# Layer 0 of a four-layer graph attention stack: biases as TensorE products, row copies on ScalarE, later input copies issued from the SP queue

## The chip, the cores and the metric

One core of one Trainium2 chip. The metric is the device time of one execution in microseconds: the median of 3 executions. The kernel before takes 3261.68 us (3260.0 to 3262.12). The profiled execution has a span of 3261.5 us.

## What is computed

The input is `x`, 3327 nodes with 256 features in f32, and one adjacency matrix of 3327 x 3327 integers, the same for four layers. Some 1% of its entries are ones, and each row has at most a few dozen. Every layer is graph attention with a residual and a layer norm. The change lies in layer 0, whose scores are of the kind in which the nonlinearity sits inside the sum over features:

```python
g_src = nodes @ W_src_w.T + W_src_b
g_tgt = nodes @ W_tgt_w.T + W_tgt_b
g = leaky_relu(g_src[:, None, :] + g_tgt[None, :, :], 0.2)
score = where(adj_mat != 0, einsum('ijc,c->ij', g, a_w), -inf)
x = layernorm(x + softmax(score, axis=1) @ g_tgt)
# layers 1 to 3: other forms of attention over the same adj, each with residual and layernorm
```

## The kernel before

**Layer 0 works on lists of neighbours.** `sparse0` (from L250) never forms the dense scores. For each node it finds the column numbers of the ones in its adjacency row (at most 56), sorts nodes by their number of neighbours, and gathers the target rows of the neighbours, k-th neighbour by k-th neighbour for 128 nodes at a time. A gather is an indirect DMA issued by POOL (L527), 923 of them for the layer.

**Tiles and sets.** The nodes are 26 tiles of 128 rows (the last has 127). They are grouped in three sets of 5, 9 and 12 tiles (`SETS`). Within a set, the nodes are ranked by their neighbour count over all the set's tiles, so that a later tile of the ranked order needs fewer gathers (`LEVELS`).

**Tables in DRAM.** `table_d` holds a target row of 260 floats for each node: `g_tgt` (256), in column 256 its share of the score that is linear in the target, and zeros. `own_d[s]`, one per set, holds what a node needs of itself: minus `g_src` (columns 0 to 255), its input row of x (256 to 511), and its target row (512 on). The copies of x into the middle columns are DRAM-to-DRAM transfers issued by POOL at L312, before anything else of the layer uses them; `copy_rows` (L104) cuts each into a multiple of 16 rows and a remainder, which makes four transfers.

**Three generators feed the tables.** `targets(it)` (L332) loads 128 columns of x transposed on SP (L322), multiplies them on TensorE into `pt` (PSUM, two buffers), then VectorE adds the bias, replicated over all partitions in `bt_row`, into `row` (L343), ScalarE copies the one column 256 (L344), and ScalarE's queue issues the two writes to the tables (L345, L346). A memset on VectorE zeroes the columns from 256 on (L336). `sources(it)` (L349) does likewise with `w_src` into `pss` (one buffer); VectorE computes `-pss - bias` in one instruction (L359), and ScalarE's queue issues the write (L363). `neighbours(s)` (L376) does the ranking of one set: for each tile it loads two halves of 128 adjacency rows on SP (L396, two `adj_i` buffers; it shows as L110, the line in `copy_rows`), turns the ones into descending numbers (L402), takes the eight largest of each chunk of 64 (L421), and then the largest 56 of what is left (L433, L435). It makes a key from the count, and TensorE replicates the keys of the tile over the partitions (`key_rows`, L466). After all tiles, L475 counts for each node how many keys are larger, and L479 makes these the ranks. `neighbours` itself advances `sources`, at half of the chunks of each half.

**The order of the work.** Within `sparse0`, TensorE, VectorE, ScalarE and POOL run in the order in which the program is written (`manual_schedule`, L259 to L266); SP isn't in this list. The first phase (L720) writes, in turn, one tile of `targets` and one step of `neighbours(0)`, then the rest of `neighbours(0)`. POOL then scatters the neighbour lists to their ranks (`write_list`, L488) and reads them back (L496). After that a loop over all parts (groups of up to 8 gathers, L770) writes for each part: as many steps of `neighbours(1)` and `neighbours(2)` as are due (L771 to L776), gathers four parts ahead, and `score`, with `combine` at the end of a tile. `lay_out` (L537) brings a node's own source row and `a_row` to PSUM on ScalarE, which also scales the gathered rows by their weights (L633); TensorE adds the scaled rows up (L636). So VectorE's single queue holds the ranking of the later sets and the scores of the current one, and POOL's holds the gathers and, when a set is ranked, its list writes.

**Afterwards.** `layers` (L973) runs layers 1 to 3, dense, on TensorE above all. If a row had more neighbours than the lists hold, a dense fallback would run (L1441); it doesn't with these inputs. One statement outside the layers is of use below: the memset of `most` at L1435, near the end of the program.

Of the kernel before, what the change touches and what calls it, by code (L numbers as in the profile page):

```python
# [8 lines left out]
F32 = mybir.dt.float32  # L9
# [5 lines left out]
ALU = mybir.AluOpType  # L15
# [4 lines left out]
P = 128  # L20
# [12 lines left out]
SETS = (5, 9, 12)  # L33
# [8 lines left out]
ROW = 260  # L42
# [4 lines left out]
def gat_stack(  # L47
# [29 lines left out]
    nc = tc.nc  # L77
    n, dim = x.shape
    nt = -(-n // P)
    kc = dim // P  # L80
# [23 lines left out]
    def copy_rows(engine, dst, src):  # L104

        rows = dst.shape[0]
        whole = rows // 16 * 16
        for lo, hi in ((0, whole), (whole, rows)):
            if lo < hi:
                engine.dma_start(dst[lo:hi], src[lo:hi])  # L110
# [7 lines left out]
    def load_row(work, src, name):  # L118

        size = src.shape[0]  # L120
        t = work.tile([P, size], F32, tag="row_" + name, name=name, bufs=1)
        nc.sync.dma_start(
            t, bass.AP(tensor=src.tensor, offset=src.offset, ap=[[0, P], [1, size]])
        )
        return t
# [124 lines left out]
    def sparse0(lost):  # L250
        GROUP, TURNS, LEAD = 8, 11, 4
        starts = [sum(SETS[:s]) for s in range(len(SETS))]
        with ExitStack() as s0:
            const0 = s0.enter_context(tc.tile_pool(name="s_const", bufs=1))
# [10 lines left out]
                )  # L265
            )  # L266

            w_tgt = const0.tile([P, kc, dim + 1], F32, name="w_tgt0")
            nc.sync.dma_start(w_tgt[:, :, :dim], w_tgt_t.rearrange("(c p) f -> p c f", p=P))
            a_row = load_row(const0, a_w, "a_row")  # L270
            bt_row = load_row(const0, b_tgt, "bt_row")
            w_src = const0.tile([P, kc, dim], F32, name="w_src0")
            nc.scalar.dma_start(w_src, w_src_t.rearrange("(c p) f -> p c f", p=P))
            bs_row = load_row(const0, b_src, "bs_row")
            for c in range(kc):
                t = io0.tile([P, dim], F32, tag="hs", name="dots0")
                nc.vector.tensor_mul(t, w_tgt[:, c, :dim], a_row)
# [4 lines left out]
            ones = const0.tile([P, P], F32, name="ones")  # L282
# [4 lines left out]
            for lo, hi in halves:  # L287
                hi = -(-hi // P) * P
# [19 lines left out]
            own_d = []  # L308
            for s, size in enumerate(SETS):
                lo, hi = starts[s] * P, min(n, (starts[s] + size) * P)  # L310
                own_d.append(dram.tile([size * P, OWN], F32, name=f"own{s}_d"))
                copy_rows(nc.gpsimd, own_d[s][: hi - lo, dim : 2 * dim], x[lo:hi, :])  # L312

            def own_rows(it):
                s = max(s for s in range(len(SETS)) if starts[s] <= it)
                at0 = (it - starts[s]) * P
                return own_d[s][at0 : at0 + P, :]

            def columns_of(it):
                pn = rows_of(it)  # L320
                xt = io0.tile([P, kc, P], F32, tag="xt", name="xt", bufs=4)
                nc.sync.dma_start(xt[:, :, :pn], x_t_p[:, :, it * P : it * P + pn])  # L322
                return xt, pn

            def project(p, xt, pn, weight):
                for k in range(kc):
                    nc.tensor.matmul(
                        p[:pn, : weight.shape[2]], xt[:, k, :pn], weight[:, k, :],
                        start=(k == 0), stop=(k == kc - 1),
                    )  # L330

            def targets(it):  # L332

                xt, pn = columns_of(it)
                row = io0.tile([P, ROW], F32, tag="row", name="row", bufs=3)
                nc.vector.memset(row[:, dim:], 0.0)  # L336
                if pn < P:
                    nc.vector.memset(row[:, :dim], 0.0)
                    nc.vector.memset(row[:, dim : dim + 1], -FAR)
                pt = ps0.tile([P, BANK], F32, tag="acc", name="pt")  # L340
                project(pt, xt, pn, w_tgt)
                yield
                nc.vector.tensor_add(row[:pn, :dim], pt[:pn, :dim], bt_row[:pn])  # L343
                nc.scalar.copy(row[:pn, dim : dim + 1], pt[:pn, dim : dim + 1])  # L344
                nc.scalar.dma_start(table_d[it * P : (it + 1) * P, :], row)  # L345
                nc.scalar.dma_start(own_rows(it)[:, 2 * dim :], row)  # L346
                yield

            def sources(it):  # L349

                xt, pn = columns_of(it)
                pss = ps0.tile([P, BANK], F32, tag="ps", name="pss", bufs=1)
                project(pss, xt, pn, w_src)
                yield
                minus = io0.tile([P, dim], F32, tag="minus", name="minus")
                if pn < P:
                    nc.vector.memset(minus, 0.0)
                    nc.scalar.dma_start(own_rows(it)[pn:, dim : 2 * dim], minus[pn:])
                nc.vector.scalar_tensor_tensor(  # L359
                    minus[:pn], pss[:pn, :dim], -1.0, bs_row[:pn],  # L360
                    op0=ALU.mult, op1=ALU.subtract,
                )
                nc.scalar.dma_start(own_rows(it)[:, :dim], minus)  # L363
                yield

# [10 lines left out]
            def neighbours(s):  # L376
# [8 lines left out]
                for t in range(size):  # L385
                    it = starts[s] + t
                    pn = rows_of(it)
                    before, of_rows = of_rows, sources(it)
                    cand = io0.tile([P, len_c, 8], F32, tag="cand", name="cand")
                    sums = io0.tile([P, 4], F32, tag="sums", name="sums")  # L390
# [95 lines left out]
            def write_list(s, t):  # L486
                ranks_i, payloads = placed[s]
                nc.gpsimd.indirect_dma_start(  # L488
                    out=lists_d[s][:, :],
                    out_offset=bass.IndirectOffsetOnAxis(ap=ranks_i[:, t : t + 1], axis=0),  # L490
                    in_=payloads[t][:, :], in_offset=None,
                )

            def read_lists(s):
                lst = io0.tile([P, max(SETS), KMAX + 2], U32, tag="lst", name="lst")
                nc.gpsimd.dma_start(  # L496
                    lst[:, : SETS[s], :], lists_d[s].rearrange("(t p) k -> p t k", p=P)
                )
                listed[s] = lst
# [221 lines left out]
            for it in range(nt):  # L721
                for _ in targets(it):
                    pass
                next(first, None)
# [27 lines left out]
            for it in range(SETS[0]):  # L752
                write_list(0, it)
            read_lists(0)


            ahead, owed, steps = [], {}, 0
# [665 lines left out]
    lost = nodes.tile([P, 2 * nt], F32, name="lost")  # L1423
    nc.vector.memset(lost, 0.0)
    sparse0(lost)
    with ExitStack() as rs:
        layers(rs)
# [75 lines left out]
```

The softmax here doesn't subtract the row's maximum and nothing guards it: scores larger than these inputs give would overflow.

## Time and profile before

| | us | share of the span |
|---|---|---|
| span | 3261.5 | |
| PE busy | 2224.4 | 68% |
| DVE (VectorE) busy | 2318.1 | 71% |
| ACT (ScalarE) busy | 741.5 | 23% |
| POOL busy | 1029.6 | 32% |
| DMA, SP's queue / POOL's queue / ScalarE's queue | | 19.8% / 16.9% / 3.2% of 16 engines |
| gathers, L527 POOL x923 | 912.6, 989 ns each | |

How to read it: the shares are means over two quite different parts. Layer 0 holds POOL's whole work; layers 1 to 3, in the second half, hold most of TensorE's. Of the stretches of layer 0:

| stretch, us | PE | DVE | ACT | POOL | DMA share |
|---|---|---|---|---|---|
| 0 to 50 | 16.48 | 25.41 | 2.40 | 7.53 | 0.74 |
| 50 to 100 | 22.61 | 43.44 | 2.07 | 0.00 | 0.67 |
| 100 to 150 | 12.74 | 45.30 | 0.96 | 3.95 | 0.46 |
| 152 to 432 | 76.32 | 248.64 | 55.19 | 180.74 | 0.54 |
| 432 to 905 | 177.63 | 458.68 | 132.38 | 349.30 | 0.53 |
| 905 to 1545 | 259.48 | 356.96 | 224.98 | 466.15 | 0.42 |

"PE", "DVE", "ACT", "POOL" and "SP" are the engines; a name with q at the end is the engine's sequencer, which issues DMAs. In a line of the timeline the columns are the start, the duration, engine, line, operation, destination and source, and the number of instructions merged; in brackets stands the idle time ahead of it and what ended it. In a line of the waits they are who waited, for whom, and then the total, the number of times and the longest.

### The profile page before, as it was taken

What the parts mean: (1) busy time and instruction counts of PE and PEld (TensorE: products, weight loads), DVE (VectorE), ACT (ScalarE), POOL (GpSimd) and SP (SyncE); (2) the same over time, 40 slices, a digit from 0 to 9 for tenths busy, and PEclk for the clock granted to TensorE, in tenths of its full rate; (3) what the DMA queues carried; (4) which work ended last, traced back from release to release, by engine and by line L of the source; (5) the groups of instructions that cost most, each with busy time, mean ns of one, the idle gap of its engine ahead of it and who ended that gap; (6) DMA issues with size and microseconds to landing.
All of it is one profiled execution on the core that took longest, in us unless ns stands there. A gap on an engine that the chain in (4) does not pass through costs nothing.

```text
span 3261.5 us, 44647 instructions
## 1 busy us (share of the span) xinstructions
PE 2224.4 (68%) x15644; PEld 1218.1 (37%) x15644; DVE 2318.1 (71%) x6589; ACT 741.5 (23%) x2002; POOL 1029.6 (32%) x1034
## 2 busy tenths in 40 slices
PE   3203332343441444343899999999999999999997
PEld 2101111121220221111478888774334444334342
DVE  6789999999975655554235642117888788899998
ACT  0003231342341343333334431110111110110110
POOL 0077657777767777774000000000000000000000
PEclk7556666666765776676699999999999999999998
DMA  7466536555435444443466753332212212212111
GB/s 216 137 141 180 169 100 150 173 157 155 112 86 109 124 111 113 113 113 91 125 199 199 201 161 93 100 99 72 63 44 68 61 46 65 63 49 57 56 47 48
DMA packets 176842, 364.21 MB, mean 112 GB/s; under 512 B 33746, under 2 KB 118964, under 8 KB 176610
## 3 DMA queue, kind: packets, MB, share of 16 engines
q1 hardware_dynamic: 96682, 183.56, 19.8%
q0 software_dynamic: 49632, 141.57, 16.9%
q10 hardware_dynamic: 30296, 36.15, 3.2%
q8 instruction: 126, 2.06, 0.3%
q14 instruction: 106, 0.87, 0.1%
HBM read 320.99 MB, written 43.58 MB: 112 GB/s over the span
## 4 chain that ended last, share of the span: by engine, by line
PE 46%; DVE 4%; DMA 2%; ACT 1%; issue 1%; DVEq 0%; SPq 0%; POOL 0%; ACTq 0%; POOLq 0%
PE acc L1198 17%; PE acc L1159 15%; PE acc L1206 8%; PE misc L1011 3%; DVE e L1075 3%; PE misc L1048 1%; DMA at_i<-in_adj_t_dram 1%; PE misc L1104 1%; DMA at<-at_d 1%; PE misc L1280 0%; PE misc L1241 0%; PE acc L636 0%; DVE stats L1355 0%; DVE h L1353 0%; ACT feat L1023 0%
## 5 line engine op out<-in xcount | busy, mean ns | idle before, releaser
L527 POOL DMA_INDIRECT g<-table_d,lst x923 | 912.6, 989 | 295.6 <-issue 268.8
L1075 DVE SCALAR_TENSOR_TENSOR e<-rate,feat,at 128x896 f32<-128x896 f32 (+4 forms) x832 | 843.1, 1078 | 67.7 <-PE acc L1206 58.4
L636 PE MATMUL acc<-g,ident 128*128 128x512 f32 (+1 forms) x934 | 454.7, 644 | 545.2 <-ACT g L633 512.7
L1198 PE MATMUL acc<-e,feat 128*32 128x384 f32 (+2 forms) x6656 | 722.8, 514 | 5.2 <-DVE e L1075 2.4
L225 POOL TENSOR_TENSOR rstds<-rstds,minus_half 128x7 f32<-128x7 f32 (+1 forms) x12 | 19.6, 1633 | 1671.7 <-DVE rstds L224 1671.7
L636 PEld LDWEIGHTS acc<-g,ident 128*128 128x128 f32 x934 | 193.3, 211 | 783.7 <-ACT g L633 561.6
L546 DVE TENSOR_TENSOR y<-g,both 128x1024 f32<-128x1024 f32 (+2 forms) x240 | 276.0, 1173 | 238.4 <-DMA g<-table_d,lst 223.5
L1206 PE MATMUL acc<-e,feat 128*32 128x384 f32 (+3 forms) x3328 | 397.5, 512 | 0.0
L1198 PEld LDWEIGHTS acc<-e,feat 128*32 128x32 f32 x6656 | 245.1, 109 | 381.8 <-issue 262.5
L633 ACT ACTIVATE g<-g,w 128x256 f32<-128x256 f32 x923 | 370.6, 494 | 0.0
L552 DVE SCALAR_TENSOR_TENSOR y<-y,both 128x256 f32<-128x256 f32 x923 | 324.5, 415 | 0.0
L1159 PE MATMUL acc<-feat,e 128*128 128x257 f32 (+2 forms) x1352 | 307.4, 381 | 0.6 <-DVE h L1173 0.6
L1159 PEld LDWEIGHTS acc<-feat,e 128*128 128x128 f32 (+2 forms) x1352 | 253.2, 190 | 39.7 <-issue 4.1
L1159 PE MATMUL acc<-feat,at 128*128 128x257 bf16 (+2 forms) x2028 | 240.9, 276 | 7.5 <-DMA at<-at_d 7.3
L466 PE MATMUL key_rows<-key_diag,ones 128*128 128x128 f32 x52 | 17.8, 440 | 314.5 <-DVE key_diag L465 259.5
L1159 PEld LDWEIGHTS <-at 128*128 128x128 bf16 (+2 forms) x2028 | 200.2, 100 | 43.9 <-DMA at<-at_d 8.0
L1075 DVE SCALAR_TENSOR_TENSOR e<-rate,feat,at_i 128x896 f32<-128x896 f32 (+2 forms) x104 | 112.2, 1081 | 143.1 <-DMA at_i<-in_adj_t_dram 109.8
L1206 PEld LDWEIGHTS acc<-e,feat 128*32 128x32 f32 (+1 forms) x3328 | 136.1, 110 | 164.2 <-issue 150.4
L421 DVE MAX8 cand<-num 128x8 f32<-128x64 uint16 x1352 | 178.9, 209 | 1.0
L542 ACT COPY both<-own_of 128x256 f32<-128x256 f32 x26 | 9.7, 374 | 602.1 <-DMA own_of<-own_d,lst 469.2
L466 PEld LDWEIGHTS key_rows<-key_diag,ones 128*128 128x128 f32 x52 | 12.1, 278 | 327.8 <-DVE key_diag L465 216.0
L1092 ACT CAST at<-at_i 128x896 bf16<-128x896 int32 (+2 forms) x104 | 92.0, 885 | 108.5 <-DMA at_i<-in_adj_t_dram 104.2
(158 smaller groups left out, 1707.5 us busy)
## 6 DMA issues: line engine op xcount, KB each, us to landing
at<-at_d SPq DMA_DIRECT2D x150, 224.0 KB
at_i<-in_adj_t_dram SPq DMA_DIRECT2D x50, 448.0 KB
adj_i<-in_adj_dram SPq DMA_DIRECT2D x25, 832.0 KB
adj_i<-in_adj_dram SPq DMA_DIRECT2D x25, 831.5 KB
g<-table_d,lst POOLq DMA_INDIRECT x923, 2.8
at<-at_d SPq DMA_DIRECT2D x75, 192.0 KB
at<-at_d SPq DMA_DIRECT2D x75, 191.8 KB
at_d<-at ACTq DMA_DIRECT2D x50, 224.0 KB
```

The source lines that it names most:

```text
L421: nc.vector.max(cand[:, lo // CHUNK + c, :], v[:, c * CHUNK : (c + 1) * CHUNK])
L527: nc.gpsimd.indirect_dma_start(out=g[:, k - k0, :], out_offset=None, in_=table_d[:, :], in_offset=bass.IndirectOffsetOnAxis(ap=entry["lst" ...
L546: nc.vector.tensor_tensor(y, rows, minus_src[:, None, :].to_broadcast([P, m, dim]), op=ALU.max)
L552: nc.vector.scalar_tensor_tensor(y, y, 1.0, a, op0=ALU.mult, op1=ALU.mult, accum_out=sc)
L633: nc.scalar.activation(rows, rows, AF.Copy, scale=w[:, k : k + 1])
L636: nc.tensor.matmul(dst, ident, rows, start=start, stop=stop)
L1011: nc.tensor.matmul(pacc[:pn, : dim + nh], ht[:, k, :pn], self.weight[:, k, :], start=(k == 0), stop=(k == kc - 1),)
L1075: nc.vector.scalar_tensor_tensor(e[:pn, : c1 - c0], self.rate[b][:pn, h_of, : c1 - c0], q, at[:pn, : c1 - c0], op0=ALU.max, op1=ALU.mult,)
L1092: nc.scalar.copy(at[:pn, :w], at_i[:pn, :w])
L1159: nc.tensor.matmul(accs[s][:pn, : dim + 1], a[:pj, s * P : s * P + pn], f[:pj, : dim + 1], start=(j == 0 and part == 0), stop=(j == nt - 1 ...
L1198: nc.tensor.matmul(accs[x][p][q : q + 32, : hi - lo], f[:pj, at0 : at0 + 32], es[at0 // hd][:pj, lo:hi], start=(j == 0), stop=(j == nt - 1),)
L1206: nc.tensor.matmul(accs[x][pairs][h_of * 32 : (h_of + 1) * 32, : hi - lo], f[:pj, dim + h_of : dim + h_of + 1].to_broadcast([pj, 32]), es[ ...
```

## The change

It has three parts.

- The biases become products. `project` takes a third, optional product of a row of ones (1 x 128) with the bias as a single row (1 x 260 or 1 x 256), accumulated into the same PSUM tile. The bias rows are loaded once to one partition instead of being replicated to 128. The target weights are widened to 260 columns with zeros, so that the product already gives the whole table row.
- ScalarE takes the rows out of PSUM. One copy of 260 columns replaces VectorE's addition, its memset of the last columns and ScalarE's one-column copy; one multiplication by -1 replaces VectorE's combined instruction for the source rows. VectorE no longer does anything in `targets` and `sources`, except for the incomplete last tile.
- Of the copies of x to the own tables, only that of set 0 stays with POOL at the start. Those of sets 1 and 2 are issued from SP, and stand in the program after the lists of set 0 are read back.

It is meant to take work from VectorE and to keep the copies of the later sets out of the start.

```diff
@@ -265,13 +265,17 @@
                 )
             )
 
-            w_tgt = const0.tile([P, kc, dim + 1], F32, name="w_tgt0")
+            w_tgt = const0.tile([P, kc, ROW], F32, name="w_tgt0")
             nc.sync.dma_start(w_tgt[:, :, :dim], w_tgt_t.rearrange("(c p) f -> p c f", p=P))
+            nc.vector.memset(w_tgt[:, :, dim:], 0.0)
             a_row = load_row(const0, a_w, "a_row")
-            bt_row = load_row(const0, b_tgt, "bt_row")
+            bt_row = const0.tile([1, ROW], F32, name="bt_row")
+            nc.vector.memset(bt_row, 0.0)
+            nc.sync.dma_start(bt_row[:, :dim], b_tgt[None])
             w_src = const0.tile([P, kc, dim], F32, name="w_src0")
             nc.scalar.dma_start(w_src, w_src_t.rearrange("(c p) f -> p c f", p=P))
-            bs_row = load_row(const0, b_src, "bs_row")
+            bs_row = const0.tile([1, dim], F32, name="bs_row")
+            nc.sync.dma_start(bs_row, b_src[None])
             for c in range(kc):
                 t = io0.tile([P, dim], F32, tag="hs", name="dots0")
                 nc.vector.tensor_mul(t, w_tgt[:, c, :dim], a_row)
@@ -309,7 +313,8 @@
             for s, size in enumerate(SETS):
                 lo, hi = starts[s] * P, min(n, (starts[s] + size) * P)
                 own_d.append(dram.tile([size * P, OWN], F32, name=f"own{s}_d"))
-                copy_rows(nc.gpsimd, own_d[s][: hi - lo, dim : 2 * dim], x[lo:hi, :])
+                if s == 0:
+                    copy_rows(nc.gpsimd, own_d[s][: hi - lo, dim : 2 * dim], x[lo:hi, :])
 
             def own_rows(it):
                 s = max(s for s in range(len(SETS)) if starts[s] <= it)
@@ -322,26 +327,28 @@
                 nc.sync.dma_start(xt[:, :, :pn], x_t_p[:, :, it * P : it * P + pn])
                 return xt, pn
 
-            def project(p, xt, pn, weight):
+            def project(p, xt, pn, weight, bias=None):
                 for k in range(kc):
                     nc.tensor.matmul(
                         p[:pn, : weight.shape[2]], xt[:, k, :pn], weight[:, k, :],
-                        start=(k == 0), stop=(k == kc - 1),
+                        start=(k == 0), stop=(k == kc - 1 and bias is None),
+                    )
+                if bias is not None:
+                    nc.tensor.matmul(
+                        p[:pn, : weight.shape[2]], ones[:1, :pn], bias, start=False, stop=True
                     )
 
             def targets(it):
 
                 xt, pn = columns_of(it)
                 row = io0.tile([P, ROW], F32, tag="row", name="row", bufs=3)
-                nc.vector.memset(row[:, dim:], 0.0)
                 if pn < P:
-                    nc.vector.memset(row[:, :dim], 0.0)
+                    nc.vector.memset(row, 0.0)
                     nc.vector.memset(row[:, dim : dim + 1], -FAR)
                 pt = ps0.tile([P, BANK], F32, tag="acc", name="pt")
-                project(pt, xt, pn, w_tgt)
+                project(pt, xt, pn, w_tgt, bt_row)
                 yield
-                nc.vector.tensor_add(row[:pn, :dim], pt[:pn, :dim], bt_row[:pn])
-                nc.scalar.copy(row[:pn, dim : dim + 1], pt[:pn, dim : dim + 1])
+                nc.scalar.copy(row[:pn], pt[:pn, :ROW])
                 nc.scalar.dma_start(table_d[it * P : (it + 1) * P, :], row)
                 nc.scalar.dma_start(own_rows(it)[:, 2 * dim :], row)
                 yield
@@ -350,16 +357,13 @@
 
                 xt, pn = columns_of(it)
                 pss = ps0.tile([P, BANK], F32, tag="ps", name="pss", bufs=1)
-                project(pss, xt, pn, w_src)
+                project(pss, xt, pn, w_src, bs_row)
                 yield
                 minus = io0.tile([P, dim], F32, tag="minus", name="minus")
                 if pn < P:
                     nc.vector.memset(minus, 0.0)
                     nc.scalar.dma_start(own_rows(it)[pn:, dim : 2 * dim], minus[pn:])
-                nc.vector.scalar_tensor_tensor(
-                    minus[:pn], pss[:pn, :dim], -1.0, bs_row[:pn],
-                    op0=ALU.mult, op1=ALU.subtract,
-                )
+                nc.scalar.mul(minus[:pn], pss[:pn, :dim], -1.0)
                 nc.scalar.dma_start(own_rows(it)[:, :dim], minus)
                 yield
 
@@ -752,6 +756,9 @@
             for it in range(SETS[0]):
                 write_list(0, it)
             read_lists(0)
+            for s in range(1, len(SETS)):
+                lo, hi = starts[s] * P, min(n, (starts[s] + SETS[s]) * P)
+                copy_rows(nc.sync, own_d[s][: hi - lo, dim : 2 * dim], x[lo:hi, :])
 
 
             ahead, owed, steps = [], {}, 0
```

## The prediction

> **What bounds the kernel now.** First the busy slices of the page, to see which engine holds which part of the span.
>
> ```profile
> DVE  6789999999975655554235642117888788899998
> ...
> POOL 0077657777767777774000000000000000000000
> ```
>
> A slice is 81.5 us. POOL works from slice 2 to slice 18, so layer 0 ends there (the chain of waits has its last write, `sums_d`, at 1541.75 us). The change touches only layer 0. Layers 1 to 3 take its output and load their own weights after it (1544.74 in the chain), so a shift of that end shifts the end of the kernel by the same amount. POOL at 7 tenths is a full engine: its gathers take 0.95 us and 0.30 us passes before each ("issue"). The question is what POOL waits for, in the waits of 0 to 170 us:
>
> ```profile
> POOL lists_d L488 <- DVE ranks_i L479: 133.7, 1, 133.7
> ...
> DVE num L402 <- DMA adj_i<-in_adj_dram: 15.5, 1, 15.5
> ...
> DVE row L343 <- PE pt L327: 11.3, 5, 2.6
> ```
>
> POOL stands until VectorE has ranked the first set (ranks at 141.35 us), and VectorE itself stands twice: 15.5 us for the first adjacency tile, and 11.3 us in L343 for the target products. After that, all that VectorE waits for between 152 and 915 us (in total, times, longest):
>
> ```profile
> DVE y_own L546 <- ACT both L543: 17.9, 1, 17.9
> DVE y L546 <- DMA g<-table_d,lst: 6.5, 2, 3.9
> DVE junk L475 <- PE key_rows L466: 3.7, 1, 3.7
> ```
>
> and two of the waits of POOL between 166 and 1512 us:
>
> ```profile
> POOL lists_d L488 <- DVE lost L574: 24.8, 1, 24.8
> ...
> POOL lists_d L488 <- DVE inv L658: 11.5, 1, 11.5
> ```
>
> From 179 to 905 us VectorE hardly waits, and POOL waits for it twice, for the lists of sets 1 and 2 (ranks at about 431 and 905 us). So layer 0's end is: VectorE's work up to 905 us, then POOL's gathers. A VectorE instruction taken out ahead of the ranks of set 2 brings the end forward, as long as POOL's two waits (24.8 and 11.5 us) are not used up.
>
> The timeline shows what one removed instruction is worth: the distance between its neighbours' starts, not its duration.
>
> ```profile
> 45.26 0.29 DVE L465 TENSOR_SCALAR key_diag<-ident,keys 128x128 f32<-128x128 f32 x1
> 45.49 0.06 DVE L336 MEMSET row<- 128x4 f32 x1
> 48.15 0.42 DVE L343 TENSOR_TENSOR row<-pt,bt_row 128x256 f32<-128x256 f32 x1 [2.59 <-PE pt L327]
> 48.49 1.88 DVE L402 SCALAR_TENSOR_TENSOR num<-adj_i,rev 128x1664 uint16<-128x1664 int32 x1
> ...
> 52.61 0.41 DVE L359 SCALAR_TENSOR_TENSOR minus<-pss,bs_row 128x256 f32<-128x256 f32 x1
> 52.94 0.42 DVE L343 TENSOR_TENSOR row<-pt,bt_row 128x256 f32<-128x256 f32 x1
> ...
> 53.27 1.73 DVE L421 MAX8 cand<-num 128x8 f32<-128x64 uint16 x13
> ```
>
> L359 costs 0.33 us; L343 with its memset costs 0.33 where it doesn't wait and 3.0 us (45.49 to 48.49) where it does.
>
> Last, the start of the timeline, for the copies and the order of SP's queue:
>
> ```profile
> 0.90 0.06 DVE L1435 MEMSET most<- 128x1 f32 x1
> ...
> 2.69 9.32 SPq L322 DMA_DIRECT2D xt<-in_x_t_dram  x6
> ...
> 4.46 3.65 POOL L110 DMA_DIRECT2D own_d<-in_x_dram  x4
> ...
> 10.98 0.44 ACTq L346 DMA_DIRECT2D own_d<-row  x1
> 12.12 0.88 SPq L110 DMA_DIRECT2D adj_i<-in_adj_dram  x2
> ```
>
> The four copies of x into the own tables are issued at 4.5, 5.4, 6.2 and 7.1 us and land 7.9, 11.4, 17.3 and 16.7 us later (12.4, 16.8, 23.5, 23.8). The adjacency load issued at 12.12 arrives at 25.8, two microseconds after them; by the windows the DMA share is 1.0 or above from 8 to 22 us.
>
> **The skill.** "DMA: Bandwidth & Descriptors", section "Queues, rings and completion order": an engine takes turns between queue rows by packet, and takes one row's descriptors in ring order. The section "Issuing engines are not separate DMA queues" adds that the issuing engine changes nothing in the bandwidth. The trace agrees: the load on SP's queue waited for copies that POOL had issued. The same page, "Anatomy of one DMA", says that a wait is taken on the issuing sequencer, before dispatch: so the row write issued at 10.98, right behind L345's (10.59 to 10.94), while the copy into the same rows landed only at 12.4, had no dependence on it; columns that don't overlap aren't ordered. "VectorE: DVE Perf Modes", section on the TRN2 errata, prices a ScalarE PSUM-to-SBUF operation at 172 cycles plus one per element at 1.2 GHz: an estimate of 0.36 us for 260 columns. The trace has 0.16 us for the one-column copy of L344 (the formula gives 0.144) and 0.376 for 256 columns from SBUF (L542). I use 0.38.
>
> **The change, part by part.**
>
> *Targets (L343, L336).* Of 26 pairs one lies ahead of the first adjacency tile and is hidden. Four wait for PE, once per tile of the set: 4 x 3.0 = 12.0 us. Nothing takes the wait's place on VectorE, which no longer reads `pt` and goes on to the next adjacency tile (loaded by then: L402 has waited for one only at the start). The other 21 give 21 x 0.34 = 7.1 us. (The zeroing of the last tile's row stays.)
>
> *Sources (L359).* Five in set 0; the last, at 136.23, lies beside the wait for `key_rows` (VectorE goes on at 137.20 because of PE), so 4 x 0.33 = 1.3 us. The 21 of sets 1 and 2 lie in the waitless stretch: 21 x 0.33 = 7.0 us, of which 9 x 0.33 = 3.0 shorten POOL's 24.8 us and 4.0 its 11.5 us. Both remain positive, so all of it counts.
>
> *PE.* The trace has four matmul records for two products (104 for 26 tiles), 0.38 to 0.64 us each, so the bias product adds two, at most 1.3 us a tile: 26 x 1.3 = 34 us beside 39 + 9 us of these products in the first 166 us. PE is idle for more than half of it, and runs up to two tiles ahead of ScalarE. Nothing, since ranking hides it.
>
> *ScalarE.* 26 x (0.38 - 0.16) + 5 x 0.38 = 7.6 us in a phase where it is busy for about 6 of 150 us. Later 21 x 0.38 = 8 us at 14 to 39% busy. The new wait: `mul` waits for PE's `pss`; behind it stand the write of `minus`, later `both` copies, exponentials and scalings. In the kernel before, that queue already waited for L359 on VectorE (it issues the write L363), so this becomes shorter. On PE, the next `pss` product waits for ScalarE, which may be in a run of scalings (27 in 10.9 us); then `key_rows` is late and L475 waits, as once already for 3.7 us. Bounds 0 to 5 us for each of two sets; I take 0, since the product is half a tile behind `mul`.
>
> *Rows for the biases.* Two loads of 128 KB become 1 KB each. Worth about 0.26 MB at 300 GB/s, 0.9 us of a saturated queue, counted below. Two short memsets are hidden behind the wait for `w_tgt`.
>
> *Copies of sets 1 and 2.* 2,687 KB of 3,327 move from POOL's queue to SP's. In the code they stand after the ranking, but SP isn't in the list of engines whose order is written by hand, and they read an input and write columns that nobody else writes: nothing holds them. The trace shows what becomes of such instructions: the memset of L1435, one of the last of the program, ran at 0.90 us, and SP has six loads of x columns, five of them later in the program, ahead of the first adjacency load. SP has a gap after the fourth of these, at about 4.3 us, until the first target product frees a buffer (8 us). I expect the copies there, so again ahead of the adjacency load. Then the same bytes still precede it, less 0.26 MB, started a little sooner; half of the second adjacency half (0.4 MB, 1 us) no longer mixes in. Gain 2 us. If they are placed behind the first two adjacency loads or where the code has them, the load is free of them: lower bound of its arrival about 16 us (issue at 12.12 and 0.83 MB behind what is queued), gain 9.5 us.
>
> Sum: 12.0 + 7.1 + 1.3 + 7.0 + 2.0 = 29.4 us. 3261.7 - 29.4 = **3232 us**, with bounds of 0 to 10 us less on ScalarE's side, and of 2 us less to 7.5 more on the copies'.
>
> **Rivals.**
>
> *The copies go behind the adjacency load* (0.28): 12.0 + 7.1 + 1.3 + 7.0 + 9.5 = 36.9, so 3225 us. For it: the code's place, and that SP may be too busy in the first microseconds. A collision at the ranks is then harmless: after its first tile of set 1 VectorE waits 17.9 us anyway. Against it: the early memset.
>
> *ScalarE or POOL keeps the later gain* (0.12): L359's 7 us are eaten by `key_rows` waiting on ScalarE, so 22.4 and 3239 us; with both waits at 5 us, 3242. For it: the 3.7 us of L475; against it: ScalarE at 14 to 39%.
>
> *The copies clog SP's queue* (0.06), slower: no row shows such a copy from SP. If each 1 KB row is a packet of 0.3 us, 2,687 rows on 16 engines take 50 us; the first adjacency tile arrives near 61, +35, minus the 27.4 of VectorE: 3269 us. Against it: the same rows, with 640 KB more, landed within 19 us of their issue on POOL's queue (4.5 to 23.8).
>
> *The early place, as above* (0.54): 3232 us.
>
> **How the numbers follow.** The range 3219 to 3243 holds the early place with ScalarE's 10 us of loss, the late place with 6 us more gain (estimates of a few instructions' spacing and of one load's arrival), and the third; outside are the clog and a leftover. Faster by over 6.5 us: 0.90; same 0.04; slower 0.06.
>
> **What would show it.** VectorE without L336, L343, L359; no wait of 2.59 us after `key_diag`; ranks of set 0 near 119 us (111 in the late case), POOL's waits for lists near 22 and 7.5 us; `own_d` copies on SP near 4 us. Wrong if the first adjacency tile arrives after 27 us, if VectorE waits for adjacency tiles again, if ScalarE's `mul` leaves `key_rows` late, or if layers 1 to 3 take longer than the 1720 us after 1541.

## The result, and the profile after

| | us | ranks of set 0 at | first adjacency tile used at |
|---|---|---|---|
| before | 3261.9 (3260.0 to 3263.55) | 141.35 | 25.82 |
| after | 3245.43 (3245.12 to 3245.74) | 131.91 | 26.00 |
| forecast | 3232 (3219 to 3243) | near 119 | some 2 us earlier |

The ratio is 0.995 (95% interval 0.9932 to 0.9967), from four executions of each kernel. The kernel is 16.5 us faster. The direction was right; the gain is 13 us smaller than the forecast 29.4, and the time lies 2.4 us above the range.

**Page, busy slices of the kernel after** (one slice is 81.1 us):

```profile
PE   7514342353451344434899999999999999999997
DVE  7699999999965565554245542117888789899998
POOL 0177667677677777774000000000000000000000
PEclk9998676676775777666899999999999999999998
```

POOL has work in slice 1 already, and the picture of layer 0 is the same. Two digits of slice 0 are odd: PE is 7 tenths busy (3 before), and the granted clock reads 9 there (7 before). TensorE has a third product for each tile, but not twice the work.

**Waits of 0 to 170 us, after** (who waited, for whom, total, times, longest):

```profile
POOL lists_d L492 <- DVE ranks_i L483: 127.0, 1, 127.0
ACT row L351 <- PE pt L337: 86.7, 23, 14.3
...
DVE num L406 <- DMA adj_i<-in_adj_dram: 16.7, 1, 16.7
...
DVE row L346 <- DMA table_d<-row: 9.9, 1, 9.9
```

VectorE's 11.3 us of waits for `pt` are gone, as predicted. The wait for the first adjacency tile is not shorter. And there is a wait that the forecast doesn't have: 9.9 us in L346, the memset of the incomplete last tile's row. `row` has three buffers, so this memset needs the one whose target tile, three before it, has been written to `table_d`. ScalarE writes it when it has copied it, and ScalarE's copy waits for TensorE in 23 cases (86.7 us).

**Timeline after, around that memset** (start, duration, engine, line, operation, number of merged instructions, and in brackets the idle time before it):

```profile
98.19 0.29 DVE L469 TENSOR_SCALAR key_diag<-ident,keys 128x128 f32<-128x128 f32 x1
98.39 1.88 DVE L406 SCALAR_TENSOR_TENSOR num<-adj_i,rev 128x1664 uint16<-128x1664 int32 x1
...
108.17 1.23 PE L337 MATMUL pt<-bt_row,ones 1*128 1x260 f32 x2
109.33 2.10 PE L332 MATMUL pt<-w_tgt,xt 128*128 128x260 f32 x4
...
111.37 1.23 PE L337 MATMUL pt<-bt_row,ones 1*128 1x260 f32 x2
112.47 0.28 DVE L346 MEMSET row<- 128x260 f32 x1 [9.88 <-DMA table_d<-row]
112.53 0.80 PE L470 MATMUL key_rows<-key_diag,ones 128*128 128x128 f32 x2
```

Where `key_diag` was followed by a 2.59 us wait, L406 now comes 0.20 us after it. But TensorE is late: the keys made at 98.19 are replicated only at 112.53, because TensorE's queue is in program order and target tiles stand ahead. A target tile takes 3.19 us from the start of one bias product to the next (108.17 to 111.37): 2.03 for four records with the weights, 1.16 for the two of the bias.

**Stretches of 18 us** (length; busy time and count of PE, PEld, DVE, ACT, POOL; granted clock; DMA share; GB/s), first of the kernel after, then of the kernel before:

```profile
80.00:98.00 18.00, 18.00 (x36) 9.97 (x36) 17.22 (x90) 2.26 (x6) 0.00 (x0) 1.00 0.70 206
98.00:116.00 18.00, 18.00 (x36) 9.29 (x34) 7.90 (x37) 1.50 (x4) 0.00 (x0) 1.00 0.64 189
```

```profile
80.00:98.00 18.00, 5.67 (x18) 4.20 (x18) 14.76 (x82) 0.64 (x4) 0.00 (x0) 0.72 0.60 171
98.00:116.00 18.00, 7.05 (x21) 4.89 (x22) 15.54 (x88) 0.80 (x5) 0.00 (x0) 0.68 0.67 206
```

TensorE is busy in every one of 18 us. 36 records in 18 us are 0.50 us each; before, 18 in 5.67 are 0.31. So twice the records take three times as long. The records of the same products in the kernel before, on PE:

```profile
75.92 1.13 PE L327 MATMUL pss<-w_src,xt 128*128 128x256 f32 x4 [1.76 <-DVE row L336]
76.89 1.03 PE L327 MATMUL pt<-w_tgt,xt 128*128 128x257 f32 x4
```

1.03 us for four records, where the kernel after needs 2.10 all the way to 116 us. The first tiles of a burst take 2.08 us before, too (the one at 36.68 us); there TensorE speeds up after a few microseconds of work, and after the change it doesn't. The granted clock contradicts this: it reads 1.00 for the stretches in which each record takes twice as long. It reads 1.00 also from 132 to 152 us, where TensorE has no product at all, so here it doesn't follow TensorE's work. The spacing of the records decides.

**POOL's waits for lists, 130 to 1545 us, after:**

```profile
POOL lists_d L492 <- DVE lost L578: 24.6, 1, 24.6
...
POOL lists_d L492 <- DVE inv L662: 7.1, 1, 7.1
```

The ranks of sets 1 and 2 are there at 419.35 and 889.45 us (431.53 and 905.26 before), so 12.2 and 15.8 us earlier; the last write of `sums_d` is at 1525.45 (1541.75), 16.3 us earlier.

**Start of the timeline, after:**

```profile
4.77 8.78 SPq L110 DMA_DIRECT2D own_d<-in_x_dram  x3
...
15.02 8.92 SPq L110 DMA_DIRECT2D adj_i<-in_adj_dram  x2
...
26.00 1.89 DVE L406 SCALAR_TENSOR_TENSOR num<-adj_i,rev 128x1664 uint16<-128x1664 int32 x1 [16.73 <-DMA adj_i<-in_adj_dram]
```

The copies of the later sets stand after the ranking in the program and are issued at 4.77 us, where the forecast expected them (about 4.3). They hold SP's sequencer for 8.78 us: the two large ones 0.6 and 0.9, the third, with its 15 rows, 7.1 us. So the adjacency load is issued at 15.02 instead of 12.12.

### The profile page after: what moved, and what is told of

Read it like the earlier page. It is cut to its first block, busy times and chain, and to the rows that moved or that the text cites. A ratio compares the mean times of both kernels' runs of the same rounds, so it can differ in the third digit from the quotient of the medians.

```text
span 3243.3 us, 44794 instructions
## 1 busy us (share of the span) xinstructions
PE 2288.7 (71%) x15748; PEld 1245.0 (38%) x15748; DVE 2301.3 (71%) x6513; ACT 755.9 (23%) x2028; POOL 1028.0 (32%) x1031
## 3 DMA queue, kind: packets, MB, share of 16 engines
q1 hardware_dynamic: 99132, 186.05, 20.4%
## 4 chain that ended last, share of the span: by engine, by line
PE 46%; DVE 4%; DMA 2%; ACT 1%; issue 1%; SPq 0%; DVEq 0%; POOL 0%; ACTq 0%; POOLq 0%
PE acc L1205 17%; PE acc L1166 15%; PE acc L1213 8%; PE misc L1018 3%; DVE e L1082 3%; PE misc L1055 1%; DMA at_i<-in_adj_t_dram 1%; DMA at<-at_d 1%; PE misc L1111 1%; PE misc L1287 0%; PE misc L1248 0%; PE acc L640 0%; DVE stats L1362 0%; DVE h L1360 0%; ACT feat L1030 0%
```

## The experiments

The theory after this reading: TensorE sets the pace of the first phase, since its records run at half speed; VectorE pays for that at the memset (9.9 us). Rivals: the moved copies delay something; ScalarE's longer copies hold the tiles; the order of TensorE's queue (a key product standing ahead of target tiles until its keys are there) makes it late. The quoted expectations call the experiments e1 to e12, in the order in which they stand here; the kernel after is the starting point of each unless its heading says otherwise.

### Leaving the bias products out

The output of this kernel lacks the biases of layer 0.

```diff
-                project(pt, xt, pn, w_tgt, bt_row)
+                project(pt, xt, pn, w_tgt)
...
-                project(pss, xt, pn, w_src, bs_row)
+                project(pss, xt, pn, w_src)
```

> The kernel after without the products with the biases (the biases of layer 0 are left out of the computation). Theory (TensorE has become the pace of the ranking): a target tile costs TensorE 2.1 us instead of 3.19, so from the first key product at 44.3 us it needs some 56 us instead of 82 for what is left, runs ahead of VectorE again, and VectorE's wait of 9.9 us in L346 goes. Ranks of set 0 near 121.5 us instead of 131.9, the whole 10 us shorter: 3235. Rival (the row buffers come free late because the writes to the tables land late, whatever TensorE does): the wait stays near 10 us, ranks near 132, 3245.

Measured: 3237.9 us, ratio 0.9929 (0.9913 to 0.9946). The first adjacency tile is used at 26.96 us and the ranks are there at 123.00: 96.0 us for the ranking, 105.9 in the kernel after, 115.5 before. No wait in L346. PE in this kernel:

```profile
45.85 4.25 PE L332 MATMUL pt<-w_tgt,xt 128*128 128x260 f32 x12
49.94 1.03 PE L332 MATMUL pss<-w_src,xt 128*128 128x256 f32 x4
```

Without the bias products TensorE speeds up to 1.03 us a tile within some 4 us. ScalarE's copies are as in the kernel after, so they aren't the cause. But this takes 1.16 us of work a tile away as well as the slow records; which of the two matters is still open.

### The memset of the last row on POOL

```diff
-                    nc.vector.memset(row, 0.0)
-                    nc.vector.memset(row[:, dim : dim + 1], -FAR)
+                    nc.gpsimd.memset(row, 0.0)
+                    nc.gpsimd.memset(row[:, dim : dim + 1], -FAR)
```

> The kernel after with the two memsets of the incomplete last row tile on POOL instead of VectorE. Theory (TensorE is the pace): VectorE's wait in L346 (9.9 us) goes, but its last wait, for key_rows at L479, grows from 0.9 to some 5 to 6 us, since TensorE can't be done with the products written ahead of it before about 122.5 us. Ranks near 127, the whole 4 to 5 us shorter: 3241. Rival (that one memset was the whole loss): ranks near 122, 3235.5.

Measured: 3241.26 us, 0.9939 (0.9922 to 0.9956). Ranks at 128.38, 101.5 us after the first tile. VectorE's waits of 0 to 170 us:

```profile
DVE num L406 <- DMA adj_i<-in_adj_dram: 20.9, 2, 17.9
...
DVE junk L479 <- PE key_rows L470: 3.6, 1, 3.6
```

With the memset gone from its queue, VectorE meets the late TensorE in other places: 3.0 us at a further adjacency tile and 3.6 us at `key_rows` (0.9 after). Only 4.4 of the 9.9 us are won. The memset was just the first instruction to feel it.

### The copies issued from ScalarE's queue

ScalarE's order is written by hand, SP's isn't.

```diff
-                copy_rows(nc.sync, own_d[s][: hi - lo, dim : 2 * dim], x[lo:hi, :])
+                copy_rows(nc.scalar, own_d[s][: hi - lo, dim : 2 * dim], x[lo:hi, :])
```

> The kernel after with the copies of sets 1 and 2 issued from ScalarE's queue at the same place of the program; that queue's order is the written one, so they really come after the ranking. Theory (the early place of the copies on SP costs the first adjacency load about 10 us): first adjacency tile used near 16 us instead of 26, everything in the ranking moves with it, since the first key product on TensorE moves too; ranks near 122.5, 3236. Rival 1 (the pace of TensorE is set from the start and not from the first key product): ranks move by less than 6 us, 3240 or more. Rival 2 (the copies then collide with the list writes): ranks near 122.5, but the first gather more than 24 us after them (23.9 in the kernel after), 3239 or more.

Measured: 3236.58 us, 0.9925 (0.9909 to 0.9942). The copies go out at 115.24 us, and VectorE's waits are:

```profile
DVE row L346 <- DMA own_d<-row: 9.8, 1, 9.8
DVE num L406 <- DMA adj_i<-in_adj_dram: 8.8, 1, 8.8
```

The first adjacency tile is used at 17.85 us, 8.2 earlier; the ranks are at 123.72, also 8.2 earlier. The L346 wait stays at 9.8, so it has nothing to do with the copies. The first gather comes 25.3 us after the ranks (25.2 in the kernel after): the late copies don't collide with the list writes.

### The key products three quarters of a tile later

```diff
-                    nc.tensor.matmul(
-                        key_rows[:, t * P : (t + 1) * P], ones, key_diag, start=True, stop=True
+                    waiting.append(
+                        lambda t=t, key_diag=key_diag: nc.tensor.matmul(
+                            key_rows[:, t * P : (t + 1) * P], ones, key_diag, start=True, stop=True
+                        )
...
+                                if b and waiting:
+                                    waiting.pop()()
```

> The kernel after with each key product written to TensorE's queue three quarters of a tile later (the last one at once). Theory (TensorE is the pace, and loses 11 us standing in front of the first key product from 33.3 to 44.3 us): it goes on with targets in that time, is 9 to 11 us ahead for the rest, and VectorE's wait of 9.9 us in L346 shrinks below 2. Ranks near 122.5, 3236. Rival (the row writes or SP's loads are the pace): nothing moves, 3245.

Measured: 3262.88 us, 1.0007 (1.0 to 1.0014). This expectation failed. In set 0 it gained 5 us (ranks at 126.80, no L346 wait, 4.6 us more for adjacency tiles). In set 1 it lost more; waits of VectorE from 135 to 925 us and of POOL from 130 to 1545:

```profile
DVE junk L485 <- PE key_rows L474: 23.3, 2, 19.3
...
POOL lists_d L498 <- DVE lost L584: 43.9, 1, 43.9
```

The edit applies to all sets. In set 1 a delayed key product falls behind the sums of a finished tile in TensorE's queue. These wait 32.4 us for the rows that ScalarE scales, start at 403.82 us and hold the queue until the key product runs at 420.85; VectorE stands 19.3 us and POOL 43.9 instead of 24.6. A product that other queues wait for isn't written behind a run of sums that has to wait itself.

### The kernel before with the copies moved, and the kernel after with them at the start

Each part alone: to the kernel before the third part of the change is added, and from the kernel after it is taken away.

```diff
 kernel before, copies moved
-                copy_rows(nc.gpsimd, own_d[s][: hi - lo, dim : 2 * dim], x[lo:hi, :])
+                if s == 0:
+                    copy_rows(nc.gpsimd, own_d[s][: hi - lo, dim : 2 * dim], x[lo:hi, :])
...
+            for s in range(1, len(SETS)):
+                lo, hi = starts[s] * P, min(n, (starts[s] + SETS[s]) * P)
+                copy_rows(nc.sync, own_d[s][: hi - lo, dim : 2 * dim], x[lo:hi, :])
 kernel after, copies back: the same lines the other way
```

> The kernel before with only the copies of sets 1 and 2 moved to SP at the place where the change puts them; all else as before. Theory (SP issues them at about 5 us, ahead of the first adjacency load, so the part brings nothing): first adjacency tile used at 26 us, as before and after; ranks 141 to 142, 3261 to 3262, no difference. Rival (they go where they are written, after the ranking): first tile used near 17 us, 9 us shorter, 3252.

> The kernel after with all copies of x on POOL at the start, as in the kernel before; the part with the bias products and ScalarE's copies alone. Theory (that part carries the whole gain): first adjacency tile used at 25 to 26 us, VectorE waits some 10 us in L346, ranks 131 to 132, 3244 to 3246. Rival (SP's early copies cost the change something, as SP stands 7 us at the third of them): first tile used near 24, 3243 or less.

Measured: 3259.46 us, 0.9993 (0.9985 to 1.0002), for the moved copies alone: first tile at 26.10, ranks at 141.66, no difference. And 3243.76 us, 0.9948 (0.9933 to 0.9963), for the rest alone: first tile at 26.21, ranks at 132.38, a 10.1 us wait of the memset. So the third part brings nothing as it is, and the other two bring all of it, with the wait.

### Late copies, memset on POOL, and the bias as two bf16 products

The bias is split into a bf16 row and a bf16 row with the remainder, each multiplied by a row of bf16 ones; this keeps about 16 bits of the bias. Of the edit only the products are shown; the copies and the memsets are as in the two experiments above.

```diff
-                    nc.tensor.matmul(
-                        p[:pn, : weight.shape[2]], ones[:1, :pn], bias, start=False, stop=True
-                    )
+                    for k in range(2):
+                        nc.tensor.matmul(
+                            p[:pn, : weight.shape[2]], ones_b[:, :pn], bias[:, k, :],
+                            start=False, stop=(k == 1),
+                        )
```

> The kernel after with the copies of sets 1 and 2 from ScalarE's queue (late), the memsets of the last row tile on POOL, and each bias product as two bf16 products (the bias as a bf16 part and the bf16 rest), which should cost TensorE some 0.5 us a tile instead of 1.2. Theory (TensorE's pace and the early copies are the two losses): first tile used near 18 us, no wait of VectorE in L346, key products never late; ranking 95 to 97 us from the first tile, ranks 113 to 115, 3228. Rival (a bf16 product costs TensorE as much as an f32 one here): VectorE waits 4 us for the key products, ranks near 119, 3232.

Measured: 3224.28 us, 0.989 (0.9875 to 0.9905), 31 to 41 us below the kernel before by the interval. First tile at 15.52, ranks at 111.17, 95.7 us apart. PE:

```profile
41.83 1.15 PE L339 MATMUL pt<-w_tgt,xt 128*128 128x260 f32 x4
42.91 0.39 PE L345 MATMUL pt<-bt_two,ones_b 1*128 1x260 bf16 x2
```

A tile takes 1.40 us (41.83 to 43.23), and TensorE runs at full speed with products over one row among the others.

### Late copies, memset on POOL, and later key products in set 0 alone

```diff
+                    if s > 0 or t == size - 1:
+                        waiting.pop()()
```

(added to the later key products; copies on ScalarE's queue and memsets on POOL as above)

> The kernel after with the copies of sets 1 and 2 from ScalarE's queue, the memsets of the last row tile on POOL, and the key products three quarters of a tile later in set 0 alone (e4 had them later in all sets). Theory (in e4 set 0 gained 5 us, and set 1 lost 19 us because the last but one key product came to stand behind the sums of a finished tile on TensorE): the loss goes, the gain stays; ranking some 100 us from the first tile at 18, ranks near 118, POOL's wait for the lists of set 1 back to 24.6 us, 3232. Rival (e4's loss has another cause): the wait for the lists of set 1 is above 40 us again, 3250.

Measured: 3236.01 us, 0.9925 (0.991 to 0.994). First tile at 17.86, ranks at 123.03: 105.2 us, where some 100 were expected, and no better than the kernel after (105.9). VectorE's wait of set 0:

```profile
DVE num L407 <- DMA adj_i<-in_adj_dram: 18.1, 4, 8.8
```

8.8 of it is the first tile; the other 9.3 us are waits for three later adjacency tiles. The loss of set 1 is gone (POOL's wait is 24.6 again), but with a better order of TensorE's queue, and with the memset out of VectorE's, the 9 us only move to the loads. A likely way, not shown by itself: SP's queue issues the x columns and the adjacency tiles in order, and the x columns wait for TensorE's buffers. TensorE works here without a break from 8 to 107 us, at 3.19 us a tile. So the order of the queue, as a rival, falls: it is TensorE's pace.

### The bias product over all 128 rows

The bias stands in the first of 128 rows and the others are zeros, against a 128 x 128 tile of ones. The result is the same, and so is the number of columns that stream; only the rows that the product addresses are 128 instead of one.

```diff
-            bt_row = const0.tile([1, ROW], F32, name="bt_row")
+            bt_row = const0.tile([P, ROW], F32, name="bt_row")
...
-                        p[:pn, : weight.shape[2]], ones[:1, :pn], bias, start=False, stop=True
+                        p[:pn, : weight.shape[2]], ones[:, :pn], bias, start=False, stop=True
```

> The kernel after with each bias product over all 128 rows of the array instead of one: 128 rows of ones times a tile that holds the bias in row 0 and zeros in the others. The result and the instructions' size stay, 260 columns in f32. Theory (a product over a single row keeps TensorE from being granted its full speed: in the kernel after it stays at half speed through the ranking, 0.51 us a product, where the kernel before and e1 fall to 0.26): TensorE speeds up a few us after each start as in e1, a target tile costs 1.6 to 1.7 us, no wait of VectorE in L346, ranks near 122, 3236. Rival 1 (the speed follows the data, and zeros count for nothing): half speed stays, 3.19 us a tile, ranks 132, 3245. Rival 2 (any third f32 product does it): as rival 1, and e10 too.

Measured: 3235.74 us, 0.9925 (0.9909 to 0.9942). First tile at 25.29, ranks at 121.35, 96.1 us, with no L346 wait. PE:

```profile
44.19 1.94 PE L333 MATMUL pt<-w_tgt,xt 128*128 128x260 f32 x4
45.92 1.07 PE L338 MATMUL pt<-bt_row,ones 128*128 128x260 f32 x2
...
48.91 1.04 PE L333 MATMUL pt<-w_tgt,xt 128*128 128x260 f32 x4
49.79 0.60 PE L338 MATMUL pt<-bt_row,ones 128*128 128x260 f32 x2
```

The same products, the same order: after 4 us the four records take 1.04 instead of 2.10 us and a tile 1.32 (48.91 to 50.23) instead of 3.19. So it isn't the added work, nor a third f32 product as such. Nor are the values the cause, since all but one row are zeros.

It isn't the chance of one execution either. From 44 to 116 us, four records of a target tile take 1.94 us or more, every time, in all seven traces with an f32 bias product over one row or 32 (the kernel after, five versions of it above, and the one over 32 rows below). In the other seven the middle value is 1.04 to 1.15 us.

### Shares of the bias in all rows, and the same with late copies

Every row holds the bias and the other operand is 1/128. This rules out that the zeros made a difference, and, with the late copies and the memset on POOL, makes a second version of the change.

```diff
+            share = const0.tile([P, P], F32, name="share")
+            nc.vector.memset(share, 1.0 / P)
...
-                        p[:pn, : weight.shape[2]], ones[:1, :pn], bias, start=False, stop=True
+                        p[:pn, : weight.shape[2]], share[:, :pn], bias, start=False, stop=True
```

> As e9, but with the bias in all 128 rows and 1/128 instead of ones, so that all rows carry data. Theory (single row): as e9, 3236. Rival 1 (the data count): full speed here and half speed in e9; 3236 here. Rival 2 (any third f32 product): half speed here too, ranks 132, 3245. The bias is loaded to 128 partitions again (as in the kernel before), which may bring the first adjacency tile up to 1 us later.

> e10 with the copies of sets 1 and 2 from ScalarE's queue and the memsets of the last row tile on POOL (as in e7, but in f32). If e10's products run at full speed: first tile used near 17 us, ranking 95 to 97 us, ranks near 113, 3225 to 3228, as e7 (3224.3). If they don't: VectorE waits 4 us for the last key product, ranks near 119, 3232.

Measured: 3239.22 us, 0.9935 (0.9919 to 0.9952), and with the late copies 3225.97 us, 0.9894 (0.9878 to 0.9911). Rankings of 96.1 us (26.24 to 122.29) and 95.6 us (17.32 to 112.95), both at full speed. The second of these, like the version with bf16 products, is about 20 us faster than the kernel after.

### The bias product over 32 rows

```diff
-                        p[:pn, : weight.shape[2]], ones[:1, :pn], bias, start=False, stop=True
+                        p[:pn, : weight.shape[2]], ones[:32, :pn], bias[:32], start=False, stop=True
```

> The bias product is taken over 32 rows (the bias in the first, zeros in 31), everything else as in the changed kernel. How many rows the clock asks for is open. If what counts is the share of the array's rows that a product keeps busy, and a quarter of them is too few, TensorE stays at 0.5 us a record: ranks of set 0 near 132, wait of the last tile's memset near 10 us, about 3245 us. If any product over clearly more than one row is enough, the records fall to 0.26 to 0.3 us after some microseconds: ranks near 122, no wait of that memset, about 3236 us. A pace between the two (tiles of 2 to 2.5 us, ranks 124 to 129) would say that the clock changes back and forth.

This one ran on another chip, on which the kernel before took 3699.4 us and this one 3696.22 (ratio 1.0002, 0.9982 to 1.0021): POOL stood up to 97 us in front of a gather there (6.5 at most in the kernel after), so the total tells nothing of the change. The phase up to the ranks shows none of this: first tile at 25.69, ranks at 131.46, and

```profile
DVE row L347 <- DMA table_d<-row: 9.7, 1, 9.7
```

```profile
70.36 2.10 PE L333 MATMUL pt<-w_tgt,xt 128*128 128x260 f32 x4
72.39 1.23 PE L338 MATMUL pt<-bt_row,ones 32*128 32x260 f32 x2
...
915.88 1.03 PE L333 MATMUL pss<-w_src,xt 128*128 128x256 f32 x4
```

as with one row. The last line shows that this chip, too, has the full pace at other times, where the queue was filled with other products. 32 rows are too few, 128 are enough; where between them the limit lies wasn't tried.

## Why the prediction was wrong in its size

**The step that failed: TensorE ("Nothing, since ranking hides it").** The size of the bias product was within its bound (1.16 us a tile against at most 1.3). Two things were wrong. The products with the weights were taken at the duration of before, but with the bias product among them they stay at the slow pace: 2.03 instead of about 1.03 us a tile. And "PE is idle for more than half of it" was read from a mean over 166 us, while TensorE's queue stands until the first key product at 44.31 us. The memset waits for the write of the target tile that ends at 109.33 us. From 44.9 us to there TensorE has 17 target tiles and 3 source tiles to do, and 20 x 3.19 = 64 us leave no room at all. At 1.32 us, as with 128 rows, they take 26. VectorE comes to the memset at 102.6 us, and the write takes 3 us, so some 55 us were free. By an estimate from these figures, either loss alone would have been hidden: slow products with the weights take 20 x 2.03 = 41 us, and a bias product of 1.16 us beside fast ones 20 x 2.19 = 44 us. What failed is that the new product's own time was counted and the pace that it leaves to the others was not.

**The sentence "Nothing takes the wait's place on VectorE", and the memset that "stays".** The four waits of L343 did vanish. But the memset that was costed at nothing because it isn't new is a different instruction afterwards: it waits for a buffer that ScalarE's write frees, and the write waits for TensorE. This costs 9.9 us. Taken away, the wait moves (3.0 + 3.6 us); with TensorE at full speed, it is gone.

**The terms that held.** Ranking from the first tile to the ranks: 115.5 before, 96.0 without the half speed, so 19.5 us for VectorE's part where 12.0 + 7.1 + 1.3 = 20.4 were forecast. L359 in sets 1 and 2: 2.7 and 3.6 us more (12.2 - 9.4, and 15.8 - 12.2) where 3.0 and 4.0 were forecast. ScalarE and POOL keep hardly anything of it; of VectorE's waits for 152 to 915 us the first three are the same as before, and the fourth ends at 914.8 us, behind the ranks of set 2 (889.45):

```profile
DVE y_own L550 <- ACT both L547: 17.4, 1, 17.4
DVE y L550 <- DMA g<-table_d,lst: 6.6, 2, 3.6
DVE junk L479 <- PE key_rows L470: 3.7, 1, 3.7
DVE hs L664 <- PE acc L640: 3.5, 1, 3.5
```

The rival in which ScalarE or POOL keeps the later gain thus falls, though its 3239 us lay nearer to the result. Of POOL's waits, the second is 7.1 us as told (near 7.5); the first is 24.6 instead of near 22, since POOL took the same 3 us already at the write of a tile's sums ahead of it (4.80 us before, 1.83 after).

**The 2.0 us at the first load.** The early place was right, the gain wasn't: the first tile comes 0.2 us later. The copy of 15 rows held SP's sequencer 7.1 us, which no part of the working looked at, but without this hold the gain is missing, too: with the copies back on POOL the adjacency load is issued at 12.93 us instead of 15.02, and its tile is used at 26.21, no earlier. The moved copies alone show no difference either. In all these kernels the bytes of the copies stand ahead of the load; why the smaller rows for the biases bring nothing stays open. Besides, the first tile is used at anything from 25.3 to 27.0 us in the kernels with early copies, so 2.0 us stand out little from the spread.

**The sum.** 29.4 - 9.9 (memset) - 2.2 (first load) - 0.9 - 0.7 (the two VectorE terms) = 15.7, against 15.8 at the ranks of set 2, 16.3 at the last `sums_d`, and 16.5 in the medians. In the version with 128 rows, where the 9.9 us are gone, the sum without them is 25.6; the medians give 24.8 (3260.53 - 3235.74; 19 to 30 by the interval).

**The rival of late copies** (3225 us, with the load at about 16 us) wasn't what happened, but it was real: put where the program has them, the copies free the load by 8.2 us, to 17.85, and give 8 to 9 us. To reach 3224 to 3226 us, it needs TensorE at full speed as well.

**The pace, as a page has it and as the traces have it.** In the Trainium skill, "TensorE: Matmul & The Clock Gate", section "What's actually happening", says that the array runs at half clock by default and gets the full one after some 3.4 us of sustained activity. The kernel before and the version with 128 rows agree (2.1 to 1.03 us a tile some 4 us into a burst). The kernel after doesn't: more than 60 us of unbroken products don't lift it, when every third one is an f32 product over one row or 32. The section "Seeing it yourself" warns that the gate's trace events are unreliable; here the record reads 1.00 over a stretch in which each record takes 0.51 us instead of 0.26. The prediction had looked for the price of the operations and not for the pace that they leave.

What is shown: at the same order and number of products, the rows that the bias product addresses decide, 128 against 1 (and 32, on another chip). What is only argued: that the gate takes account of how much of the array a stream of products uses. What is open: why the bf16 products over one row don't hold it down. They take 0.32 of 1.40 us a tile, against 1.16 of 3.19; their share, their type and their length weren't separated.

## What to carry to other kernels

A product over few rows isn't only its own time: ask what it does to the products around it, and read the pace from the spacing of the records. If a bias must go through TensorE, give its product all 128 rows; the two bf16 products over one row did as well here, for a reason that is open. And the instruction that was left alone is to be costed again when what frees its buffer changes owner, as the last tile's memset was; "idle for more than half" must be read in the stretch between the time TensorE can start and the time its results are due.

## What the hardware did that was not expected

- An f32 product over one row (or 32), every third, holds TensorE at 0.51 us a record of 260 columns from 44 to 116 us; over 128 rows the records fall to 0.26 after some 4 us.
- The recorded clock is 1.00 there, and still 1.00 from 132 to 152 us, where TensorE has no product; the version with 128 rows reads 0.50 in that stretch, without a product as well. Taken over the span, the mean reads 0.866 in the kernel after and 0.838 in the version with 128 rows, though TensorE is faster in the latter.
- A third DRAM-to-DRAM copy in a row, 15 rows long, holds SP's sequencer 7.1 us (from 6.4 to 13.5 us), where the two large ones before it took 0.6 and 0.9. It took 6.4 us on SP in the kernel before with the copies moved, and 5.0 us on ScalarE's queue.
